# Attention: middle sums of outer operands 1 and 2 on GpSimd, and one in four long scaling rows on ScalarE

## The chip, the cores and the metric

The kernel runs on one core of a Trainium2 chip. The metric is the time of one execution in microseconds (us) on the device. All data is float32. The engines are named as in the profile: PE (TensorE, matrix products; PEld are its weight loads), DVE (VectorE), ACT (ScalarE), POOL (GpSimd) and SP (the queue that issues most of the DMAs).

## What is computed

Four sequences of 512 tokens with 1024 features are normalised, sent through causal attention and, beside it, through a linear layer with a routed low-rank part; both results are added to the input.

```python
x = hidden                                    # (4, 512, 1024)
xn = layernorm(x)
x = x + attn(xn, w_qkv, w_o) + ffn(xn, W, b, A, B, gate_w, gate_b)

def attn(h, w_qkv, w_o):                      # 32 heads, 8 key/value heads, D = 128, groups of 4
    qkv = h @ w_qkv
    scores = einsum('bqhgd,bkhd->bhgqk', q, k) * D ** -0.5
    bias = where(rel >= 0, -slopes * sqrt(max(rel, 0)), -inf)   # rel = query - key position
    attn = softmax(scores + bias)
    out = einsum('bhgqk,bkhd->bqhgd', attn, v)
    return out @ w_o
```

## The kernel before

The large matrix products (the projection by `w_qkv`, and the last stage by `w_o` and `W` together) are each made by a two-level scheme of the Strassen kind: seven products of sums of quarters in place of eight products of quarters, once over outer quarters and again over inner ones. So operands have to be summed ahead of the products. The attention stage lies between the two large products, and besides attention it makes those sums of its own output that the last stage will multiply, and stores them to HBM in `s_d`.

**Units and steps.** A unit is one key/value head `h` of one sequence 2p + bi: 2 x 8 x 2 = 32 units, and the two with the same `(p, h)` follow each other and are called a pair. A unit has NQ = 4 steps, so the loop at L1221 runs over STEPS = 128 steps and six more. One step T handles two slices of 32 queries for 4 heads at once (128 partitions). Each slice has its keys in a long and a short row of scores, which fold the causal triangle: widths 512 - 32s and 32 + 32s for slice s, so a step always has 1088 columns in four rows (`rows`, L1039; k = 0 and 2 are long, 1 and 3 short).

**What a step issues, in this order.** Every engine's order is the program's order in this stage (`manual_schedule`, L1215).

1. At T % 4 = 0 the key and query loads of the next unit (SP); at T % 4 = 2 the loads of the values, half of them on POOL's queue and half on SP's (L1035), and the bias row of the next pair (ACT).
2. Ten steps after a unit's first (T % 4 = 2 too), `settle` (L1122) copies its finished output from PSUM to `O[u]` (ACT), and its sums are put in line: see below.
3. `scores(T)`: for each row a product on PE into one of four PSUM banks, bias and row minimum on DVE (L1058, result `low`), the exponential with its row sum on ACT (L1061). After the second row DVE inverts the sums of the step before (`tot`, L1069).
4. `scaled(T - 1)`: the rows of the step before times their inverse sums, in place: the short ones on ACT (L1075), the long ones on POOL (L1077).
5. `turn(T - 2)`: DVE transposes the rows of two steps before in blocks of 32 (L1086) into `pt`.
6. In odd steps `weigh` of two steps (PE, L1102): the weighted sums of the values.
7. `aside(beside, 1)` and `aside(below, ...)`: so many sums from two lists of generators. `beside` holds sums that DVE makes, `below` those that POOL makes.

**The sums.** `outer_sums` (L1136) takes the outputs of both units of a pair and makes the outer operands 5, 6 and 3, and 7 in place, by 8 instructions of 128x512 (`HEADS`: two halves of four) on POOL. `middle_sums` (L1155) makes, from outer operands, the sums that the inner level needs: four instructions for each group, s1, s2, s4 and s3, followed by the stores into `s_d`. There are three groups per pair: operands 1 and 2 (from `O` of the even unit, 128x512, with `kept` true: s3 goes to a new place, since the quarter that it would overwrite is still used by `outer_sums`; the unchanged quarters are stored ahead of the sums, L1176 and L1177), operands 5, 6 and 3 (from `OS`, 128x768), and operands 7 and 4 (from `O` of the odd unit, 128x512). L137 and L140 are the helpers `add` and `sub`, so these instructions stand under those two lines and are told apart by their tiles: `ot` is the result of middle sums, `os` and `o` those of outer sums.

Line 1170 chooses the engine of middle sums: POOL for operands 7 and 4, DVE for the other two groups. `of_pair` (L1202) is one generator: eight outer sums, then it puts operands 5, 6 and 3 in line in `beside`, then runs operands 7 and 4 itself. The step loop takes one sum per step from `beside` and one or two (even and odd steps) from `below`: in the eight steps of a pair 8 from `beside` (4 + 4 are put in) and 12 from `below` (12 are put in). From step 128 on, up to four are taken from each per step.

At step 112 the loop also asks for the first operands of the last stage (`front[0]`, L1231, 3.2 MB on SP's queue); at step 130 for the second ones.

Of the kernel before, what the change touches and what calls it, by code (L numbers as in the profile page):

```python
# [66 lines left out]
def kernel(  # L67
# [13 lines left out]
    nc = tc.nc  # L81
# [54 lines left out]
    def add(eng, dst, u, v):  # L136
        return eng.tensor_tensor(dst, u, v, ALU.add)  # L137

    def sub(eng, dst, u, v):
        return eng.tensor_tensor(dst, u, v, ALU.subtract)  # L140
# [830 lines left out]
    def attend(front, begin):  # L971
# [3 lines left out]
        with ExitStack() as stack:  # L975
# [4 lines left out]
            STEPS = len(units) * NQ  # L980
# [10 lines left out]
            def buf(tag, name):  # L991
                where = sq if tag in queries else sp if tag in passing else sb
                return where.tile([P, *sizes[tag]], F32, tag=tag, name=name, bufs=counts.get(tag, 1))

            Q, K, V, O, bias = {}, {}, {}, {}, {}
# [4 lines left out]
            def load(u, queue=nc.sync):  # L1000
                p, h, bi = u
                n = label(u)
                K[u] = buf("k", f"k_{n}")
                Q[u] = buf("q", f"q_{n}")
                queue.dma_start(out=K[u], in_=k_d[2 * p + bi, h - h % 2][:, h % 2])
                queue.dma_start(out=Q[u], in_=q_d[2 * p + bi, h])
# [17 lines left out]
            def distances(u):  # L1024
                p, h, bi = u
                t = buf("bias", f"bias_{p}_{h}")
                nc.scalar.activation(t, dist, AF.Identity, scale=slope[:, h : h + 1])
                bias[p, h] = t

            def values(u):  # L1030
                p, h, bi = u
                V[u] = buf("v" + "xy"[bi], f"v_{label(u)}")
                src = v_d[2 * p + bi, h - h % 2][h % 2].rearrange("k g c d -> k (g c) d")
                for g in range(G):
                    (nc.gpsimd, nc.sync)[g // 2].dma_start(out=V[u][ts(g, C)], in_=src)  # L1035
# [3 lines left out]
            def rows(T):  # L1039

                for e in range(2):
                    s = 2 * (T % NQ) + e
                    high = (NB - s) * C
                    yield 2 * e, PR[T][:, e, :high], high
                    yield 2 * e + 1, PR[T][:, e, high:], (s + 1) * C
# [21 lines left out]
            def inverse(T):  # L1067
                if 0 <= T < STEPS:
                    nc.vector.reciprocal(TOT[T], TOT[T])  # L1069

            def scaled(T):
                for k, row, n in rows(T):
                    by = TOT[T][:, k : k + 1]
                    if k % 2:
                        nc.scalar.activation(row, row, AF.Identity, scale=by)  # L1075
                    else:
                        nc.gpsimd.tensor_scalar(row, row, by, 1.0, ALU.mult, ALU.mult)  # L1077
# [44 lines left out]
            def settle(u, part=slice(0, 2)):  # L1122

                if u not in O:
                    O[u] = buf("o", f"o_{label(u)}")
                for g in range(G):
                    at = slice((2 - part.stop) * HS, (2 - part.start) * HS)
                    to = O[u][:, g, part.start * HS : part.stop * HS]
                    nc.scalar.copy(
                        to.rearrange("p (j k) -> p j k", k=C)[:, ::-1],  # L1130
                        PO[u, g][:, at].rearrange("p (j k) -> p j k", k=C),
                    )
# [22 lines left out]
            def middle_sums(p, h, which, of, t, kept):  # L1155


                g = len(which)
                a = t.rearrange("p (g e) (r k) -> p g e r k", g=g, r=2) if of == "o" else t.rearrange(
                    "p g e (r k) -> p g e r k", r=2  # L1160
                )
                a11, a12, a21, a22 = [a[:, :, e, r] for r in range(2) for e in range(2)]
                n = f"{p}_{h}_{which[0]}"
                m = spare.pop(which[0]) if (p, h) == last and which[0] in spare else buf(
                    f"ot{which[0]}", f"ot_{n}"
                )
                m = m.rearrange("p (s g) k -> p s g k", g=g)
                s1, s2, s4 = [m[:, k] for k in range(3)]
                s3 = m[:, 3] if kept else a21
                eng = nc.gpsimd if of == "o" and not kept else nc.vector  # L1170
                kb, kp = divmod(h + 2, KB)

                d = [s_d[i][:, :, p, kb, kp] for i in which]
                if kept:
                    for k in range(g):
                        nc.sync.dma_start(out=d[k][:, 0:4:2], in_=a[:, k, :, 0])  # L1176
                        nc.sync.dma_start(out=d[k][:, 3], in_=a[:, k, 1, 1])  # L1177
                add(eng, s1, a21, a22)
                yield
                sub(eng, s2, s1, a11)  # L1180
                yield
                sub(eng, s4, a12, s2)
                yield
                sub(eng, s3, a11, a21)
                for k in range(g):
                    if kept:
                        nc.sync.dma_start(out=d[k][:, 1], in_=s3[:, k])
                    else:
                        nc.sync.dma_start(out=d[k][:, :4], in_=a[:, k].rearrange("p e r k -> p (e r) k"))
                    nc.sync.dma_start(out=d[k][:, 4:], in_=m[:, :3, k])  # L1190
                yield

            beside, below, spare = deque(), deque(), {}

            def aside(steps, times):
                while steps and times:
                    if next(steps[0], True):
                        steps.popleft()
                    else:
                        times -= 1  # L1200

            def of_pair(p, h, eng, cuts):  # L1202

                yield from outer_sums(p, h, eng, cuts)
                beside.append(middle_sums(p, h, (5, 6, 3), "os", OS.pop((p, h)), False))
                yield from middle_sums(p, h, (7, 4), "o", O[p, h, 1], False)
# [14 lines left out]
            for T in range(STEPS + 6):  # L1221
                n, q = divmod(T, NQ)
                done, part = divmod(T - 10, NQ)
                if q == 0 and 0 < n and n + 1 < len(units):
                    load(units[n + 1])
                if q == 2 and n < len(units):
                    values(units[n])
                    if n + 1 < len(units) and units[n + 1][2] == 0:
                        distances(units[n + 1])
                if T == 112:  # L1230
                    front[0]()  # L1231
                if part == 0 and done >= 0:
                    u = p, h, bi = units[done]
                    settle(u)
                    if bi == 0:
                        beside.append(middle_sums(p, h, (1, 2), "o", O[u], True))
                    else:
                        below.append(of_pair(p, h, nc.gpsimd, HEADS))
                if T < STEPS:
                    scores(T)  # L1240
                else:
                    inverse(T - 1)
                if 0 < T <= STEPS:
                    scaled(T - 1)
                if 1 < T <= STEPS + 1:
                    turn(T - 2)
                if T == STEPS + 2:
                    earlier.__exit__(None, None, None)
                    early.__exit__(None, None, None)
                    front[1](O[units[-2]][:, :])  # L1250
                if T == STEPS:
                    fill = begin()
                if T >= STEPS:
                    for _ in range(6):
                        next(fill, None)
                for k in range(T - 7, T - 5) if T % 2 and T < STEPS else [T - 6] if T >= STEPS else []:
                    weigh(k)
                aside(beside, 1 if T < STEPS else 4)
                aside(below, 1 + T % 2 if T < STEPS else 4)
                if T == STEPS + 4:  # L1260
                    settle(units[-1], slice(1, 2))
            for _ in fill:
# [3 lines left out]
            p, h = last  # L1266
# [473 lines left out]
    def begin():  # L1740

        bank = rotation(a=(0,), b=(1,))
        for kind, rc in (("a", (0, 0)), ("b", (0, 1))):
            begun[rc] = bank(kind, "begun")[:, :HS]
            yield from ops[0].plain(*rc, begun[rc])
# [53 lines left out]
```

## Time and profile before

| | us |
|---|---|
| runs (3): median, lowest, highest | 2529.05, 2528.04, 2530.84 |
| profiled execution | 2522.98 |
| its span, first to last instruction | 2521.2 |
| PE, DVE, POOL, ACT busy in the span | 2424.5, 1838.4, 1832.5, 590.7 |
| first and last scaling row on POOL (L1077) start at | 1139.7, 1690.1 |

The granted clock of PE is 0.991 on the mean. DMA moves 681.92 MB, 270 GB/s over the span. In the profile each instruction group is named by its line, engine, operation and tiles, with shapes as partitions x elements. "Idle before" is the time that the engine stood still ahead of an instruction, and the arrow names what ended it. A busy PE is not PE at its peak, since the products overlap; the starts on its timeline tell more than the busy time. The share of a whole run also mixes three stages with different limits (projection to 1139 us, attention, last stage from about 1700), so the attention stage is to be read by itself.

### The profile page before, as it was taken

What the parts mean: (1) busy time and instruction counts of PE and PEld (TensorE: products, weight loads), DVE (VectorE), ACT (ScalarE), POOL (GpSimd) and SP (SyncE); (2) the same over time, 40 slices, a digit from 0 to 9 for tenths busy, and PEclk for the clock granted to TensorE, in tenths of its full rate; (3) what the DMA queues carried; (4) which work ended last, traced back from release to release, by engine and by line L of the source; (5) the groups of instructions that cost most, each with busy time, mean ns of one, the idle gap of its engine ahead of it and who ended that gap; (6) DMA issues with size and microseconds to landing.
All of it is one profiled execution on the core that took longest, in us unless ns stands there. A gap on an engine that the chain in (4) does not pass through costs nothing.

```text
span 2521.2 us, 44416 instructions
## 1 busy us (share of the span) xinstructions
PE 2424.5 (96%) x16096; PEld 2067.5 (82%) x16096; DVE 1838.4 (73%) x3586; ACT 590.7 (23%) x1814; POOL 1832.5 (73%) x1876
## 2 busy tenths in 40 slices
PE   7999999999899999999999999995999999999999
PEld 6888888888788888887777777774888888888887
DVE  7776677678566676757999999976765666656574
ACT  3111111110000000018777777750000000000000
POOL 4588787877698888874888878873775667647593
PEclk9999999999999999999999999998999999999999
DMA  4389898878986777747899999999887877879884
GB/s 147 109 250 326 271 334 253 263 222 260 309 253 215 240 228 230 253 126 197 261 321 317 317 329 326 317 324 344 293 317 268 327 291 288 307 267 330 309 331 149
DMA packets 517196, 681.92 MB, mean 270 GB/s; under 512 B 155817, under 2 KB 428969, under 8 KB 502770
## 3 DMA queue, kind: packets, MB, share of 16 engines
q1 hardware_dynamic: 443122, 579.45, 69.4%
q10 hardware_dynamic: 70752, 82.85, 9.9%
q0 software_dynamic: 3104, 16.78, 2.6%
q8 instruction: 128, 2.10, 0.3%
q14 instruction: 90, 0.74, 0.1%
HBM read 417.89 MB, written 261.10 MB: 269 GB/s over the span
## 4 chain that ended last, share of the span: by engine, by line
PE 57%; DVE 6%; ACT 5%; issue 4%; DMA 2%; SPq 1%; POOL 0%; DVEq 0%; ACTq 0%; POOLq 0%
PE pc L1378 16%; PE pd L1378 8%; PE pc_q L569 7%; PE po L1102 5%; PE pa L1378 4%; PE psc L1053 4%; PE pd_q L569 4%; PE pc_kv L569 3%; ACT p L1061 3%; DVE p L1058 3%; PE pa_q L569 2%; PE pd_kv L569 2%; DVE pt L1086 2%; ACT p L1075 1%; PE pa_kv L569 1%
## 5 line engine op out<-in xcount | busy, mean ns | idle before, releaser
L1061 ACT ACTIVATE p<-p,low 128x512 f32<-128x512 f32 (+15 forms) x512 | 261.0, 514 | 134.5 <-DVE low L1058 132.5
L140 POOL TENSOR_TENSOR t<-w 128x640 f32<-128x640 f32 x95 | 183.5, 1932 | 148.4 <-DMA w<-in_w_o_dram 63.8
L1053 PE MATMUL psc<-k,q 128*128 128x512 f32 (+15 forms) x1024 | 270.4, 412 | 19.2 <-DVE low L1058 18.7
L1102 PE MATMUL po<-pt,v 32*128 32x256 f32 (+7 forms) x6144 | 280.1, 332 | 4.3 <-DMA v<-v 3.8
L1102 PEld LDWEIGHTS po<-pt,v 32*128 32x128 f32 x6144 | 255.2, 187 | 27.7 <-ACT p L1061 11.1
L1053 PEld LDWEIGHTS psc<-k,q 128*128 128x128 f32 x1024 | 170.4, 190 | 112.1 <-issue 55.0
L1077 POOL TENSOR_SCALAR p<-p,tot 128x512 f32<-128x512 f32 (+7 forms) x256 | 151.3, 603 | 122.3 <-DVE tot L1069 119.6
L140 POOL TENSOR_TENSOR t<-w,t 128x640 f32<-128x640 f32 x95 | 202.3, 2129 | 33.2 <-PE pc L1378 29.4
L1058 DVE CUSTOM_DVE_ANT_0 p<-psc,bias 128x512 f32<-128x512 f32 (+15 forms) x512 | 200.3, 426 | 22.5 <-PE psc L1053 20.5
L140 POOL TENSOR_TENSOR wr<-wr 128x256 f32<-128x256 f32 x220 | 173.8, 792 | 42.3 <-DMA wr<-in_w_o_dram 16.7
L569 PE MATMUL pc_q<-xi,ti_q 128*128 128x256 f32 x640 | 165.2, 381 | 3.5 <-DVE q L137 1.7
L1086 DVE STREAM_TRANSPOSE pt<-p 128x1088 f32<-128x1088 f32 x128 | 166.6, 1301 | 0.4 <-POOL p L1077 0.4
L140 POOL TENSOR_TENSOR ti_q<-w_q 128x256 f32<-128x256 f32 x128 | 103.7, 810 | 68.4 <-PE pc_q L569 35.7
L179 ACT COPY m<-pc 128x256 f32<-128x256 f32 x30 | 11.2, 372 | 584.1 <-PE pc L1378 577.1
L140 DVE TENSOR_TENSOR wr<-wr 128x256 f32<-128x256 f32 x220 | 139.4, 634 | 7.0 <-DMA wr<-in_wt_dram 6.2
L569 PEld LDWEIGHTS pc_q<-xi,ti_q 128*128 128x128 f32 x640 | 120.2, 190 | 23.2 <-issue 3.3
L1378 PE MATMUL pc<-sa,w 128*128 128x256 f32 x480 | 113.2, 383 | 19.9 <-DMA sa<-s 19.9
L569 PE MATMUL pd_q<-xi,ti_q 128*128 128x256 f32 x448 | 118.1, 387 | 13.8 <-POOL ti_q L140 13.5
L1378 PEld LDWEIGHTS pc<-sa,w 128*128 128x128 f32 x480 | 91.8, 193 | 32.7 <-issue 20.3
L1378 PE MATMUL pc<-s,t 128*128 128x256 f32 x480 | 113.0, 383 | 5.9 <-DVE m L137 5.9
L140 POOL TENSOR_TENSOR ti_q<-w_q,ti_q 128x256 f32<-128x256 f32 x128 | 108.4, 847 | 5.0
L1378 PE MATMUL pd<-s,t 128*128 128x256 f32 x480 | 111.4, 379 | 0.0
(349 smaller groups left out, 5848.2 us busy)
## 6 DMA issues: line engine op xcount, KB each, us to landing
sa<-s SPq DMA_DIRECT2D x98, 640.0 KB, 8.0
s<-ot SPq DMA_DIRECT2D x107, 384.0 KB, 7.0
m<-wr SPq DMA_DIRECT2D x70, 512.0 KB, 4.1
w<-m SPq DMA_DIRECT2D x28, 1280.0 KB, 7.6
w_q<-in_w_qkv_dram SPq DMA_DIRECT2D x16, 2048.0 KB, 12.0
q<-q SPq DMA_DIRECT2D x32, 1024.0 KB, 8.0
s<-os SPq DMA_DIRECT2D x48, 512.0 KB, 6.3
t<-wr SPq DMA_DIRECT2D x40, 512.0 KB, 4.2
```

The source lines that it names most:

```text
L140: return eng.tensor_tensor(dst, u, v, ALU.subtract)
L179: nc.scalar.copy(dst, alike(src, dst))
L569: nc.tensor.matmul(dst, ops_w[m][:, c, :], XI[i][m][:, c, :], start=start and c == 0, stop=c == 1, skip_group_check=True,)
L1053: nc.tensor.matmul(sc[:, :n], Q[u][:, n // C - 1].rearrange("p g k -> p (g k)"), K[u][:, :n], start=True, stop=True,)
L1058: nc.vector.tensor_tensor_reduce(row, sc[:, :n], bias[p, h][:, S - n :], -SCALE, BIG, ALU.add, ALU.min, low)
L1061: nc.scalar.activation(row, row, AF.Exp, bias=low, scale=-1.0, accum_out=TOT[T][:, k : k + 1])
L1075: nc.scalar.activation(row, row, AF.Identity, scale=by)
L1077: nc.gpsimd.tensor_scalar(row, row, by, 1.0, ALU.mult, ALU.mult)
L1086: nc.vector.transpose(dst, PR.pop(T).rearrange("p s (t k) -> p s t k", k=C))
L1102: nc.tensor.matmul(PO[u, g][:, to : to + n * C].rearrange("p (n k) -> p n k", k=C), V[u][ts(g, C), b % G * NT + b // G], x[:, :, :C], star ...
L1378: nc.tensor.matmul(bk, w[:, k], x[:, k], start=start and k == 0, stop=stop and k == KB - 1, skip_group_check=True,)
```

## The change

Three edits, all in `attend`.

```diff
@@ scaled(T), L1071
                 for k, row, n in rows(T):
                     by = TOT[T][:, k : k + 1]
-                    if k % 2:
+                    if k % 2 or k // 2 and T % 2:
                         nc.scalar.activation(row, row, AF.Identity, scale=by)
                     else:
                         nc.gpsimd.tensor_scalar(row, row, by, 1.0, ALU.mult, ALU.mult)
@@ middle_sums, L1170
-                eng = nc.gpsimd if of == "o" and not kept else nc.vector
+                eng = nc.gpsimd if of == "o" else nc.vector
@@ the step loop, L1236 and L1259
                     if bi == 0:
-                        beside.append(middle_sums(p, h, (1, 2), "o", O[u], True))
+                        below.append(middle_sums(p, h, (1, 2), "o", O[u], True))
                     else:
                         below.append(of_pair(p, h, nc.gpsimd, HEADS))
...
                 aside(beside, 1 if T < STEPS else 4)
-                aside(below, 1 + T % 2 if T < STEPS else 4)
+                aside(below, 2 if T < STEPS else 4)
```

- The second long row (k = 2) of odd steps is scaled by ACT instead of POOL: in a unit the rows of slices 3 and 7, 416 and 288 wide. The other three long rows of every two steps stay on POOL.
- The middle sums of operands 1 and 2 are issued on POOL instead of DVE, four instructions of 128x512 per pair.
- They wait in POOL's list `below`, behind operands 7 and 4 of the pair before, and that list gives two sums in every step: 16 in the eight steps of a pair, and 4 + 12 are put in. The list `beside` is left with operands 5, 6 and 3, which so start as soon as they are put in line, in steps 5 to 8 after the odd unit was settled, where they ran in steps 8 to 11.

The same arithmetic is done, and the same bytes are stored.

## Prediction

> **What bounds the kernel now.** I read the busy share of 40 slices first, to find where the edited code runs, then the table of busy time by stretch, then the timelines of PE, VectorE (DVE) and GpSimd (POOL) in that stretch, then the waits and the groups by shape. The edit touches only the attention loop, from 1139 to 1724 us.
>
> ```profile
> PE   7999999999899999999999999995999999999999
> DVE  7776677678566676757999999976765666656574
> POOL 4588787877698888874888878873775667647593
> ...
> 1225.40:1609.20 383.80, 370.01 (x4933) 290.64 (x4930) 383.66 (x969) 287.64 (x979) 311.90 (x352) 1.00 1.00 321
> ```
>
> The slices show PE full almost everywhere; only in slices 20 to 26 is DVE full as well. The last line (PE, weight loads, DVE, ACT, POOL, then clock, DMA share, GB/s) covers loop steps 24 to 111, 22 units of four steps. DVE is idle for 0.14 of 383.8 us, POOL for 72, ACT for 96. A unit takes 383.8 / 22 = 17.45 us, a pair 34.9. So DVE sets the pace here; PE's 96% has to be checked against a stretch where DVE is not full:
>
> ```profile
> 1171.64 4.28 PE L1102 MATMUL po<-pt,v 32*128 32x256 f32 x96
> 1175.85 4.27 PE L1053 MATMUL psc<-k,q 128*128 128x512 f32 x16
> 1180.05 4.31 PE L1102 MATMUL po<-pt,v 32*128 32x256 f32 x96
> 1184.29 3.93 PE L1053 MATMUL psc<-k,q 128*128 128x384 f32 x16
> 1188.16 4.28 PE L1102 MATMUL po<-pt,v 32*128 32x256 f32 x96
> ...
> 1259.93 2.32 PE L1053 MATMUL psc<-k,q 128*128 128x512 f32 x8
> 1263.00 2.16 PE L1053 MATMUL psc<-k,q 128*128 128x448 f32 x8 [0.74 <-DVE low L1058]
> ```
>
> From 1171.64 to 1188.16, before DVE has its full load, one unit takes 16.52 us with no gap: PE's own floor. Later PE waits in every unit for DVE to empty the score banks. The most that a lighter DVE can give is 17.45 - 16.52 = 0.93 us per unit.
>
> **The removed DVE work.** Per pair four sums leave DVE. Their rows in steps 24 to 111:
>
> ```profile
> L137 DVE TENSOR_TENSOR ot<-o x11: 2505/2512/2523, 1238.5 to 1587.6; 128x512 f32<-128x512 f32 x11
> L140 DVE TENSOR_TENSOR ot<-ot,o x11: 1151/1154/1157, 1243.7 to 1592.8; 128x512 f32<-128x512 f32 x11
> L140 DVE TENSOR_TENSOR ot<-o,ot x11: 1240/1244/1252, 1247.5 to 1596.6; 128x512 f32<-128x512 f32 x11
> L140 DVE TENSOR_TENSOR ot<-o x11: 1364/1366/1371, 1251.4 to 1600.5; 128x512 f32<-128x512 f32 x11
> ```
>
> 2.51 + 1.15 + 1.24 + 1.37 = 6.27 us; by starts on the timeline (instructions overlap a little) 6.06. The same sums take 0.65 each at the end of the loop, where POOL is not working beside them: most of their time is waiting for POOL. DVE falls to 34.9 - 6.06 = 28.8 us per pair, under PE's 33.04.
>
> The sums that stay on DVE (operands 5, 6 and 3; 6.85 us by starts) move three steps earlier, since their queue is no longer shared: steps 5 to 8 after the odd unit is settled, instead of 8 to 11. They stay bunched in four steps: 11.04 us of other DVE work per unit plus 6.85 is 17.9 against PE's 16.52. Bounds: 0.95 each (their fastest) gives 14.8; 2.62 each (their slowest) gives 21.5. PE covers about 3.5 us of lateness: in the PE-bound stretch DVE frees a score bank at about 1197.3 and PE needs it at 1200.8. So 17.9 is covered, 21.5 would stall PE 1.5 us per pair. I take 0.
>
> **The added POOL work.** POOL is busy 311.90 / 11 = 28.35 us per pair and waits 6.4 (its scaling row waits for DVE's `tot` 73.4 us in 1200 to 1600, 11.46 pairs).
> - Removed: four long rows, 416 and 288 wide, two of each: 2 x (604 + 524 ns) = 2.26.
> - Added: four sums. POOL's own sums of this shape show both ends: 1.27 when alone, 1.72 when a DVE sum delays them. 5.1 to 6.9.
> - Removed: two POOL sums that the departing DVE sums delay, 2 x 0.45 = 0.9, or nothing if others delay them.
>
> Sum: 30.3 to 33.0 us per pair. Even the upper end is just inside PE's 33.04, with no room for waits. I take the middle, 31.6, because only four DVE sums are left to delay sixteen POOL sums. A step now has two sums and 1 or 2 rows; the pace of sums (2 x 8) equals their supply (4 + 12), so no queue grows. Rows reach the transpose late only if POOL is over 2.7 us behind (row done 1195.5, transposed 1198.25); behind the row waits the transpose, and all of DVE behind that. In the pace above POOL lags by 1 to 2 us, when the two V loads that it issues (1.04 us per unit) and a contended sum fall together.
>
> GPSIMD Engine Reference (Trainium skill), section "Performance versus the Vector engine", speaks against the move: an elementwise add of two tensors is 1.96 times slower there, so "use DVE for elementwise". The rows give 1.27 against 0.65 without company, the same ratio, and by that the change adds 2.5 us of work per pair; but by the rows with company DVE gives up 6.06 and POOL takes 5.1 to 6.9, so the ratio does not decide.
>
> **ACT.** It gains the four rows. No 416- or 288-wide scaling is in the trace; the nearest rows are its exponentials of those widths, 626 and 520 ns, so 2.29 per pair, on 26.1 now: 28.4 of 33.04. Bounds: hidden, or wholly on the path, 2.29 per pair. I take hidden: the rows come after the step's exponentials, and on the timeline ACT waits 0.9 to 2.3 us for `low` in three steps of four. In the first steps that cover is missing (ACT 9.66 of 10 us busy from 1140 to 1150): three rows there, 2 x 0.63 + 0.52 = 1.8 us lost.
>
> **Queues and DMA.** No DMA is added. The four loads-out of unchanged quarters move two steps later; the last ones stay in their step but now wait for POOL's sum, which ends up to 3.5 us into the next step. Behind them on SP's queue stand the V loads, which have five steps (some 20 us) less about 7 to land: cost nothing. If that cover goes, the price is seen at step 116:
>
> ```profile
> 1636.28 1.40 SPq L1035 DMA_DIRECT2D v<-v  x2
> ...
> 1643.40 1.19 PE L1102 MATMUL po<-pt,v 32*128 32x256 f32 x2 [3.00 <-DMA v<-v]
> ...
> 1645.35 6.38 PE L1102 MATMUL po<-pt,v 32*128 32x256 f32 x90 [0.76 <-DMA v<-v]
> ```
>
> There the block of 96 took from 1639.70 to 1651.66, 11.96 us instead of 4.21. The six stores ahead of that V load (1619.88 to 1636.1) are the ones that move three steps earlier, so 0 to 7.75 us may come back. I take 0: from 1640 to 1757 DMA is at a share of 1.0, PE waits 20 us for `sa` loads at the end of it, and what PE gains earlier it would wait longer there.
>
> The bytes set a floor too: 321 GB/s x 383.8 us = 123.2 MB. In stretches of 10 us with a share of 1.0 or more the rates are 324 to 365, mean about 339; 123.2 MB at 339 is 363 us, 16.5 per unit, level with PE. The small DMA gaps that are left (0.83 to 0.96 in one such stretch of three) would have to close. DMA: Bandwidth & Descriptors (Trainium skill), section "Specifications", puts HBM at about 358 GB/s per core; at that, by estimate, the floor were 344 us and DMA would leave 4% to spare, which no long stretch here shows.
>
> **Sum.** PE and DMA both allow 16.5 per unit; I take 16.7, adding 0.2 for the DMA gaps and the bunched DVE sums. 23 units (steps 24 to 115) x (17.45 - 16.70) = 17.2, less 1.8 at the start: 15.4 us off the profiled 2521.2 span (2522.98 with what lies around it). That execution is 6.1 under the median of the runs, 2529.05; I take the difference from the median: **2513.6**. Own range: at 16.52 with nothing lost 21 to 25, at 17.0 only 8: 2505 to 2521.
>
> **Rivals.**
> 1. *All comes back* (0.13): 23 x 0.93 = 21.4 and the 7.75 at step 116: 2500. For it: the stores move ahead of the load. Against: DMA full behind it.
> 2. *Transfers set the pace* (0.15): DMA's share is already 1.00 at 321 GB/s. If 327 is all that it sustains, 123.2 MB take 377 us: 7 saved, 1.8 lost, 2524; at 321, 2531. I put it at 2525. Against: 20-us stretches at 339 to 345.
> 3. *GpSimd sets the pace, slower* (0.17): its waits for `tot` are not slack if DVE, held back by denser POOL work, gives `tot` later. With contended sums (33.0) and half the waits kept (3.2) a pair takes 36.2, 1.3 more: x 11.5 = 15, near 2544. It decides from about 2 us of waits kept on top of 33. For it: the 2.5-us sums show DVE held through two POOL instructions. Against: two sums per step leave POOL behind `tot`, not ahead of it, and after two-sum steps it does not wait today.
>
> That the edit does nothing has no place: its three lines change engines and pace in every pair.
>
> **Chances.** Forecast 0.55. Faster by over 0.2% (5 us, about what a measurement here can tell): 0.55 + 0.13 + a third of rival 2, 0.72; within: 0.11; slower: 0.17. The range 2500 to 2533 leaves out most of rival 3 and the lower half of rival 1.
>
> **What would show it.** Right: DVE's busy time in steps 24 to 111 falls from 100% to about 87%, units near 16.7 us, POOL at 94% with waits for `tot` under 1.5 us per pair, DMA above 330 GB/s. Wrong: units over 17.4, transposes waiting for `p` of L1077 or L1075, remaining DVE sums over 2.5 us each, PE waiting for v, q or k in more places than step 116.

## The result, and the profile after

| | before | after |
|---|---|---|
| runs (4 each): median, lowest, highest | 2529.08, 2528.04, 2530.84 us | 2549.78, 2543.44, 2552.03 us |
| profiled execution, its span | 2522.98, 2521.2 us | 2549.02, 2547.2 us |
| steps 24 to 111 | 383.6 us, 17.44 per unit | 403.4 us, 18.33 per unit |

The kernel became **slower by 0.8%**: the ratio of times is 1.0077 (interval 1.0058 to 1.0096). The forecast of 2513.6 us was wrong in sign, and the time lies outside its range.

The busy shares of the 40 slices after the change, in tenths:

```profile
PE   7999999999899999999999999985999999999999
DVE  7776676678576667657777877775765766655574
POOL 4588787786698989876888988874765667656593
```

DVE has lost its full slices 20 to 26, as forecast, and POOL is fuller there. By that row alone the change works. The table of the stretch from 1225.40 to 1609.20 us (length, then busy PE, weight loads, DVE, ACT, POOL, then clock, DMA share, GB/s) says otherwise:

```profile
1225.40:1609.20 383.80, 358.44 (x4684) 280.18 (x4680) 299.78 (x888) 294.62 (x977) 327.33 (x337) 0.96 0.98 308
```

DVE is busy for 78%, POOL for 85%, PE for 93%, and transfers fell from 321 to 308 GB/s: none of these engines is full, and all have less to do per microsecond. So something late holds them all. What that is, the longest waits of PE, DVE and POOL from 1225 to 1600 us show (total us, times, longest):

```profile
DVE p L1058 <- PE psc L1053: 76.6, 39, 7.6
POOL p L1077 <- DVE tot L1069: 42.8, 19, 6.3
PE psc L1053 <- DMA q<-q: 12.6, 5, 5.1
PE psc L1053 <- issue: 10.8, 3, 4.7
```

DVE waits for PE now. POOL's waits for `tot` went down from 68.4 us in the same stretch, where rival 3 needed them to decide. PE itself waits for a load of queries, for which it never waited here before; on its timeline (start, duration, instruction, idle before):

```profile
1226.81 4.27 PE L1053 MATMUL psc<-k,q 128*128 128x512 f32 x16
1231.01 4.31 PE L1102 MATMUL po<-pt,v 32*128 32x256 f32 x96
1235.25 3.93 PE L1053 MATMUL psc<-k,q 128*128 128x384 f32 x16
1239.11 4.28 PE L1102 MATMUL po<-pt,v 32*128 32x256 f32 x96
1248.11 6.47 PE L1053 MATMUL psc<-k,q 128*128 128x512 f32 x16 [4.72 <-issue]
...
1321.63 7.25 PE L1053 MATMUL psc<-k,q 128*128 128x512 f32 x16 [3.58 <-DMA q<-q]
```

Step 24 starts at 1226.81. Its unit runs at PE's floor and would end at 1239.11 + 4.28 = 1243.39; step 28 starts at 1248.11, and its 16 products take 6.47 us in place of 4.27. That wait bears the name "issue": the trace names nothing that ended it. Five waits at the same place in other units are named `q`, and SP's queue shows the query load of step 28 late as well:

```profile
1225.15 0.91 SPq L1189 DMA_DIRECT2D s<-os  x1
1226.10 0.91 SPq L1190 DMA_DIRECT2D s<-ot  x1
1227.05 0.59 SPq L1189 DMA_DIRECT2D s<-os  x1
1228.33 0.52 SPq L1190 DMA_DIRECT2D s<-ot  x1
1228.89 1.63 SPq L1189 DMA_DIRECT2D s<-os  x1
1230.57 3.14 SPq L1190 DMA_DIRECT2D s<-ot  x1
1233.80 0.86 SPq L1005 DMA_DIRECT2D k<-k  x1
1234.71 0.45 SPq L1006 DMA_DIRECT2D q<-q  x1
```

Keys and queries have two buffers, so the load of the next unit can go only when the last scores of the unit before are made, 3.7 us ahead of step 24 (in step 16 it went then, with nothing in front of it). Here the query load went 7.9 us into the step, behind the six stores of operands 5, 6 and 3 (3 x (512 + 384) KB). A query load takes 9.0 us to land at the median and 12.3 at most (7.4 and 8.9 before; the trace has the landing of six loads in each kernel), and the unit that it must be ready for could start 16.5 us after step 24.

**Where the time went.** The two executions differ by 26.0 us of span: 1.4 before step 24, 19.8 in steps 24 to 111, 4.1 from there to the end of the wait for `sa` that opens the last stage (at 1784.24 against 1758.97; the wait is 21.79 us against 19.93), and 0.7 behind it. In steps 24 to 111 the load of the next unit goes behind the stores of 5, 6 and 3 in every second unit, eleven of 22. In five of these (steps 24, 40, 56, 72 and 88) it went 7.0 to 8.3 us into the step: they take 18.1 to 21.7 us, together 19.8 over a floor of 16.515, and the five units after them 10.0 over it. All 22 are 40 over.

### The profile page after: what moved, and what is told of

It is laid out like the page before. It is cut to its first block, busy times and chain, and to the rows that moved or that the text cites. A ratio compares the mean times of both kernels' runs of the same rounds, so it can differ in the third digit from the quotient of the medians.

```text
span 2547.2 us, 44424 instructions
## 1 busy us (share of the span) xinstructions
PE 2432.1 (95%) x16096; PEld 2070.5 (81%) x16096; DVE 1754.7 (69%) x3522; ACT 620.0 (24%) x1878; POOL 1881.4 (74%) x1876
## 4 chain that ended last, share of the span: by engine, by line
PE 48%; DMA 7%; SPq 3%; POOL 3%; ACT 2%; issue 2%; DVE 2%; DVEq 0%; POOLq 0%; ACTq 0%
PE pc L1378 16%; PE pd L1378 8%; PE psc L1053 5%; PE po L1102 5%; PE pa L1378 4%; PE pc_q L569 4%; DMA q<-q 3%; PE pd_q L569 2%; PE pc_kv L569 2%; SPq L1190 1%; ACT p L1061 1%; DMA s<-o 1%; DMA s<-ot 1%; PE pa_q L569 1%; DVE p L1058 1%
## 5 line engine op out<-in xcount | busy, mean ns | idle before, releaser
L1053 PE MATMUL psc<-k,q 128*128 128x512 f32 (+15 forms) x1024 | 279.4, 426 | 41.7 <-DMA q<-q 23.6
L1058 DVE CUSTOM_DVE_ANT_0 p<-psc,bias 128x512 f32<-128x512 f32 (+15 forms) x512 | 202.4, 432 | 127.4 <-PE psc L1053 119.0
L1053 PEld LDWEIGHTS psc<-k,q 128*128 128x128 f32 x1024 | 175.6, 198 | 139.1 <-issue 93.7
L1077 POOL TENSOR_SCALAR p<-p,tot 128x512 f32<-128x512 f32 (+2 forms) x192 | 116.5, 615 | 97.4 <-DVE tot L1069 86.6
L1075 ACT ACTIVATE p<-p,tot 128x32 f32<-128x32 f32 (+4 forms) x320 | 121.4, 439 | 0.0
L1378 PEld LDWEIGHTS pc<-sa,w 128*128 128x128 f32 x480 | 91.8, 193 | 35.6 <-issue 22.2
```

The costliest lines, as they stand in the source:

```text
L1053: nc.tensor.matmul(sc[:, :n], Q[u][:, n // C - 1].rearrange("p g k -> p (g k)"), K[u][:, :n], start=True, stop=True,)
L1058: nc.vector.tensor_tensor_reduce(row, sc[:, :n], bias[p, h][:, S - n :], -SCALE, BIG, ALU.add, ALU.min, low)
L1378: nc.tensor.matmul(bk, w[:, k], x[:, k], start=start and k == 0, stop=stop and k == KB - 1, skip_group_check=True,)
```

## The experiments

Three theories were set against each other. O: the **order** on SP's queue, stores issued ahead of the key and query loads. D: the **transfers** as a whole are too many or too dense, whatever their order. P: **GpSimd** sets the pace. O2 and P2 are the forms that O and P took after the first four runs. A ratio is to the kernel before, run beside them on the same chip (its medians there were 2527.77, 2527.99 and 2527.65 us for the three batches).

To follow O, call S the step in which a pair's odd unit is settled (S % 8 = 6). Key and query loads go out in steps S + 2, S + 6 and S + 10. Before, the stores of (7, 4) were issued from step S + 7 and those of (5, 6, 3) from S + 11, each just **behind** a load. With two sums in every step and `beside` left to (5, 6, 3), they are issued from S + 5 and S + 8, **ahead** of the loads of S + 6 and S + 10.

### First batch: undo one part, or do one part alone

**The sums of 5, 6 and 3 three steps later**, the rest as changed:

```diff
-                beside.append(middle_sums(p, h, (5, 6, 3), "os", OS.pop((p, h)), False))
+                beside.append(later(3, middle_sums(p, h, (5, 6, 3), "os", OS.pop((p, h)), False)))
```

> The changed kernel with one part undone: the sums of operands 5, 6 and 3 start three steps later, in steps 8 to 11 after the odd unit was settled as before the change; their six stores then stand on SP's queue ahead of a V load again and no longer ahead of a key and query load. Theory O (order: the query load of every second unit lands late because those stores were moved right in front of it): the waits for q (23.6 us named in the changed kernel's profile) go to under 3 us, a unit takes 16.5 to 17.0 us, total 2508 to 2520. Theory D (capacity: at PE's pace the transfers can't be served, whatever their order): loads stay late, total 2540 or more. Theory P (POOL runs late, its sums hold up SP's queue): no change, 2545 to 2552.

Measured: 2546.81 us (2540.16 to 2549.03), ratio 1.0070 (1.0054 to 1.0086). The number is D's and P's, and not O's. SP's queue shows why:

```profile
1357.76 0.38 SPq L1189 DMA_DIRECT2D s<-o  x1
1358.18 0.51 SPq L1190 DMA_DIRECT2D s<-ot  x1
1358.79 1.16 SPq L1189 DMA_DIRECT2D s<-o  x1
1359.99 1.24 SPq L1190 DMA_DIRECT2D s<-ot  x1
1361.33 1.19 SPq L1005 DMA_DIRECT2D k<-k  x1
1362.57 1.11 SPq L1006 DMA_DIRECT2D q<-q  x1
```

The load behind (5, 6, 3) goes in time now, but the other load, of S + 6, goes behind the four stores of (7, 4), and PE waits there:

```profile
1373.63 5.93 PE L1053 MATMUL psc<-k,q 128*128 128x512 f32 x16 [2.47 <-DMA q<-q]
```

One of two groups was out of the way and the loss moved to the other. The run doesn't tell O from D or P; it said that both groups must be dealt with.

**Key and query loads on ACT's queue**, past all stores:

```diff
-                    load(units[n + 1])
+                    load(units[n + 1], nc.scalar)
```

> The changed kernel with the key and query loads issued on ACT's queue instead of SP's, stores left where they are. Theory O: the load is no longer behind the six stores on its queue, but shares the DMA engines with them: waits for q under 8 us, total 2510 to 2525. Theory D: loads stay late, 2540 or more. Theory P: SP's waits for POOL no longer hold the load, 2510 to 2525 as well; so this run with the one before tells P from O.

Measured: 2517.63 us (2514.41 to 2521.38), ratio 0.9960 (0.9947 to 0.9973). The same work and the same bytes, in the same order but for these two loads, and 32 us less: no wait for `q`, 16.83 us per unit (mean of the 22 units from step 24 on, here and below), and transfers at 334 GB/s where the changed kernel had 308. That speaks for O, and against D: denser transfers went faster.

**The scaling edit alone** (the kernel before, with its line 1074 as changed):

```diff
-                    if k % 2:
+                    if k % 2 or k // 2 and T % 2:
```

> The kernel before with the scaling edit alone (one in four long rows on ACT). DVE keeps all its sums, so the unit stays near 17.4 us: total 2525 to 2531 under all theories (1.8 us lost in the first steps on ACT, up to 3 won where DVE's sums find POOL idle).

Measured: **2502.59 us** (2502.06 to 2507.71), ratio 0.9904 (0.9890 to 0.9919). Missed: 25 us faster where none were expected. Its table for the same stretch:

```profile
1225.40:1609.20 383.80, 383.80 (x5172) 304.54 (x5170) 374.99 (x1024) 326.76 (x1079) 306.42 (x326) 1.00 1.04 337
```

PE never stops: units of 16.515 us, its floor, with the middle sums still on DVE. 337 GB/s held over 383.8 us ends rival 2 and D. DVE is busy for 375 us of 384, with the work of 23.2 units where it had that of 22. The sums by shape (least/median/most ns) show how it found the room:

```profile
L137 DVE TENSOR_TENSOR ot<-o x12: 1759/1766/1776, 1237.3 to 1600.6; 128x512 f32<-128x512 f32 x12
L140 DVE TENSOR_TENSOR ot<-o,ot x12: 647/650/651, 1245.7 to 1609.0; 128x512 f32<-128x512 f32 x12
L137 DVE TENSOR_TENSOR ot<-os x11: 1484/1499/1505, 1253.8 to 1584.1; 128x768 f32<-128x768 f32 x11
L140 DVE TENSOR_TENSOR ot<-os,ot x12: 914/917/919, 1229.2 to 1592.5; 128x768 f32<-128x768 f32 x12
```

The four took 2.51, 1.24, 2.61 and 1.51 us before; the other four of a pair kept their times within 0.02. That is 0.75 + 0.59 + 1.11 + 0.59 = 3.04 us per pair, 1.5 per unit, off an engine that was full: 17.45 - 1.5 = 15.9 (and 374.99 / 23.2 = 16.1), below PE's 16.5. POOL runs one row fewer in odd steps, so the DVE sum that stands waiting behind POOL's rows is released a row earlier. First before, then with the scaling edit:

```profile
1238.03 1.22 POOL L1077 TENSOR_SCALAR p<-p,tot 128x448 f32<-128x448 f32 x2
1238.52 2.52 DVE L137 TENSOR_TENSOR ot<-o 128x512 f32<-128x512 f32 x1
1239.23 1.26 POOL L140 TENSOR_TENSOR os<-os,o 128x512 f32<-128x512 f32 x1
...
1236.60 0.65 POOL L1077 TENSOR_SCALAR p<-p,tot 128x448 f32<-128x448 f32 x1
1237.21 1.27 POOL L140 TENSOR_TENSOR os<-os,o 128x512 f32<-128x512 f32 x1
1237.27 1.78 DVE L137 TENSOR_TENSOR ot<-o 128x512 f32<-128x512 f32 x1
```

In both, the DVE sum ends 0.55 to 0.57 us after POOL's sum does. Before, it had also stood through what was left of two rows.

**The moved sums without the scaling edit** (the changed kernel, L1074 as before):

```diff
-                    if k % 2 or k // 2 and T % 2:
+                    if k % 2:
```

> The changed kernel without the scaling edit: all long rows on POOL, which then has 2.26 us more per pair. Theories O and D: within 4 us of the changed kernel, 2543 to 2554, since the loads decide. Theory P: slower than the changed kernel by up to 2.26 x 11.5 = 26 us, 2560 or more.

Measured: 2564.05 us (2559.15 to 2565.13), ratio 1.0144 (1.0127 to 1.0161). The number is P's. But PE again waits for `q`, and SP stands for 91.7 us waiting for POOL's `o` ahead of stores (84.6 in the changed kernel): POOL, with more to do, makes the sums later, and the loads behind their stores go later still. So P seems to have a part in the size, through the queue of O (the second batch takes this up).

### Second batch: is it the order?

**Stores of both groups issued just behind the key and query load** (the changed kernel; `stores` holds the six lines of L1185 to L1190, and `holding` is true up to step 116):

```diff
+                if kept or not holding[0]:
+                    stores()
+                else:
+                    held.append(stores)
...
+                if q == 0:
+                    while held:
+                        held.pop(0)()
+                holding[0] = T < 116
```

> The changed kernel, same engines and same sums at the same steps; only the stores of operands 7 and 4 and of 5, 6 and 3 are issued behind the next key and query load on SP's queue (one and two steps later) instead of ahead of it. Theory O2 (any group of stores that stands ahead of a key and query load holds it back, first until its last sum is done and then by its own transfer; with the change both groups stand there, and undoing one only moved the late load to the other): waits for q under 3 us in steps 24 to 111, a unit 16.5 to 16.9 us, total 2505 to 2522. Theory P2 (the lag of POOL stalls PE and DVE directly, the late loads are a sign of it): the total stays over 2535.

Measured: 2523.43 us (2518.67 to 2525.10, 10 runs), ratio 0.9979 (0.9969 to 0.9988). In steps 24 to 111 the loss is gone:

```profile
1225.40:1609.20 383.80, 380.59 (x5146) 301.66 (x5145) 323.67 (x959) 320.52 (x1068) 357.52 (x368) 1.00 1.03 334
```

A unit takes 16.77 us, no wait for `q` is left, DVE is at 84% and POOL at 93%. What is left above the floor stands in the odd units of the pairs (16.9 to 17.3 us, the others 16.5). In ten of these eleven DVE waits 1.6 to 2.5 us ahead of its first sum of 5, 6 and 3, seven times by name for stores that still read that buffer (`DVE ot L137 <- DMA s<-ot: 14.8, 7, 2.5`). With the loads on ACT's queue, where no store is held, such waits stand in the odd units too (nine), so the holding alone does not explain them; no run separates this rest. The time missed O2's range by a microsecond for one wait of 11.26 us ahead of step 124 (at 1666.82), after the holding has ended and while the operands of the last stage are loaded.

**The pace alone, on the scaling edit alone**: nothing is moved to POOL, only `below` gives two sums in every step, so that (7, 4) come two steps earlier:

```diff
-                aside(below, 1 + T % 2 if T < STEPS else 4)
+                aside(below, 2 if T < STEPS else 4)
```

> The kernel before with the scaling edit, and with two sums per step from POOL's list as in the change, but no sum changes its engine: operands 7 and 4 are then done and stored two steps earlier, ahead of a key and query load. POOL's work is the same as in the scaling edit alone (2502.6). Theory O2: late loads in every second unit, q waits of 10 us or more in 1225 to 1600, total 2520 to 2545. Theory P2: POOL has the room, so 2500 to 2508.

Measured: **2579.51 us** (2577.97 to 2584.37), ratio 1.0206 (1.0191 to 1.0222): 77 us slower than without this line. P2 is refuted; O2's direction is right and its size far too small. SP's queue and PE (the step began at 1323.52):

```profile
1323.52 2.58 SPq L1035 DMA_DIRECT2D v<-v  x2
...
1328.60 1.02 SPq L1189 DMA_DIRECT2D s<-o  x1
1329.66 0.56 SPq L1190 DMA_DIRECT2D s<-ot  x1
1330.26 1.52 SPq L1189 DMA_DIRECT2D s<-o  x1
1331.83 0.94 SPq L1190 DMA_DIRECT2D s<-ot  x1
1332.86 1.16 SPq L1005 DMA_DIRECT2D k<-k  x1
1334.06 1.41 SPq L1006 DMA_DIRECT2D q<-q  x1
```

```profile
1336.17 4.28 PE L1102 MATMUL po<-pt,v 32*128 32x256 f32 x96
1344.60 6.75 PE L1053 MATMUL psc<-k,q 128*128 128x512 f32 x16 [4.16 <-DMA q<-q]
```

The query load goes 10.5 us into the step and PE stands still for 4.16. With the scaling edit alone, the same two loads stand ahead of the four stores (the step began at 1307.63):

```profile
1312.98 0.52 SPq L1005 DMA_DIRECT2D k<-k  x1
1313.55 1.44 SPq L1006 DMA_DIRECT2D q<-q  x1
...
1319.12 1.06 SPq L1189 DMA_DIRECT2D s<-o  x1
...
1322.60 1.38 SPq L1190 DMA_DIRECT2D s<-ot  x1
```

Read off such timelines for all 22 units from step 24 on, from the start of a unit to the query load issued in it, for the later loads (every second unit), and the length of that unit in us:

| kernel | the later of the loads | that unit | the other units |
|---|---|---|---|
| before | 5.8 to 6.8 us (eleven) | 17.3 | 17.2 to 17.6 |
| scaling edit alone | 5.6 to 6.8 us (eleven) | 16.5 | 16.5 |
| changed kernel | 7.0 to 8.3 us (five), 5.0 to 6.9 (six) | 18.1 to 21.7, 16.5 to 19.0 | 17.1 to 19.5 |
| scaling edit and pace | 9.2 to 10.5 us (eleven) | 19.8 to 21.6 | 17.2 to 19.7 |

With the scaling edit alone 6.8 us costs nothing; from 7.0 on PE waits every time. In between it hangs on the landing: in the changed kernel four of the six loads at 5.0 to 6.9 us were followed by waits of 0.7 to 2.4 us, and two of these four took 11.5 and 12.3 us to land. So before the change the later loads had little to spare already. A unit after a long one is mostly long too.

**The scaling edit with key and query loads on ACT's queue** (both lines are shown above):

> The kernel before with the scaling edit, and the key and query loads on ACT's queue. No stores stand ahead of these loads in the steady steps, so both theories expect little there: 2498 to 2506; the one q wait near step 116 (behind the operands of the last stage) goes, up to 5 us.

Measured: 2530.76 us (2524.65 to 2537.04, 10 runs), ratio 1.0011 (1.0001 to 1.0020). Missed by 25 us. On this order the loads were in time anyway, and on ACT they hold up its exponentials: in step 48, which began at 1318.84, the first one starts only behind the query load.

```profile
1323.90 0.33 ACTq L1006 DMA_DIRECT2D q<-q  x1
1324.35 0.72 ACT L1061 ACTIVATE p<-p,low 128x512 f32<-128x512 f32 x1 [4.66 <-DVE low L1058]
```

Its input `low` was made by 1320.8. The waits of 1225 to 1600 us:

```profile
POOL p L1077 <- DVE tot L1069: 90.7, 43, 4.4
ACT p L1061 <- DVE low L1058: 45.9, 36, 5.0
...
DVE tot L1069 <- ACT p L1061: 20.9, 10, 2.8
```

DVE, which has only 9 us to spare here, waits 20.9 us for ACT. So that queue is not a free way round: it took 32 us off the changed kernel and put 28 on this one. DMA: Bandwidth & Descriptors (Trainium skill), section "Issuing engines are not separate DMA queues", says that issuing from several engines saves only the sequencer's time of issuing, usually small. Here what is saved is the time that a load stands behind stores and their waits, 2549.78 against 2517.63 us, and it is not small; that no rate is won agrees, with 334 GB/s at most on two queues and 334 to 337 on SP's alone in the kernels without waits for `q`.

**The moved sums without the scaling edit, loads on ACT's queue:**

> The change without its scaling edit, key and query loads on ACT's queue. What is left of the loss here is not the queue's: theory O2 expects 2515 to 2530 (POOL has 2.26 us more per pair than with the scaling edit, where the same queue gave 2517.6), theory P2 2540 or more.

Measured: 2525.86 us (2522.05 to 2533.40, 10 runs), ratio 0.9996 (0.9983 to 1.0009), as O2 expected: 38 us under the same kernel with the loads on SP. POOL is busy for 374.08 us of 383.8, 97%, and still no slower than before. With these loads on ACT's queue, leaving out the scaling edit costs 8.2 us (2525.86 against 2517.63), on SP's 14.3: so P seems to have a part of its own, some 8 us, beside the one through the queue.

### Third batch: one group at a time, and a better kernel

**The pace alone, on the kernel before** (the one line of the pace, nothing else):

> The kernel before with two sums per step from POOL's list as the only edit. Theory O2: the stores of operands 7 and 4 stand ahead of a key and query load, so q waits in every second unit, though at the slower pace of 17.45 us per unit there is more time for each load: 2540 to 2575. If the order of these stores did not matter, 2525 to 2531.

Measured: 2586.70 us (2585.67 to 2593.02), ratio 1.0240 (1.0225 to 1.0255). No sum and no row changes its engine, and the kernel loses 59 us, more than expected: 36.6 us of waits for `q`, nine of them, in 1225 to 1600 us, at a granted clock of 0.94. That is about three times the loss of the whole change by the line that the prediction priced at nothing.

**The scaling edit and the pace, with the stores of (7, 4) alone put behind the load:**

> The slow kernel of the second batch (scaling edit, two sums per step, no sum on another engine; 2579.5) with one difference: the four stores of operands 7 and 4 are issued one step later, behind the key and query load instead of ahead of it. The sums run at the same steps on the same engines. Theory O2: back to the scaling edit alone, 2500 to 2512, no q waits in steps 24 to 111. If the earlier sums themselves cost the time (POOL denser, DVE held longer), 2560 or more stays.

Measured: 2521.51 us (2517.99 to 2523.02, 10 runs), ratio 0.9975 (0.9966 to 0.9985). 58 of the 77 us come back by issuing four stores later, and no wait for `q` is left. The rest, expected back too, did not come: a unit takes 17.04 us, with DVE at 364.5 of 383.8. Unlike with the scaling edit alone, PE waits once per unit for DVE here (`PE psc L1053 <- DVE low L1058: 6.3, 22, 0.4`), and POOL stands 21.1 us for PE ahead of its V loads. What holds the remaining half microsecond was not taken apart: 58 of the 77 us are the order of these stores, for 19 the cause is open.

**The scaling edit, with the operands of the last stage asked for one at a time** in steps 112, 116, 120 and 124:

```diff
-                if T == 112:
-                    front[0]()
+                if T in (112, 116, 120, 124):
+                    front[0]((*QUARTERS[:3], "w")[(T - 112) // 4])
```

> The scaling edit alone (2502.6), and the first operands of the last stage are asked for one by one at steps 112, 116, 120 and 124 instead of all at step 112. The 6.5 us wait for v at step 116 and the slower products behind it should go: up to 9 us, 2493 to 2502; if the transfers behind it only move the wait to the last stage, 2500 to 2504.

Measured: **2500.67 us** (2499.12 to 2502.29), ratio 0.9894 (0.9879 to 0.9909), the fastest of all. The wait for `v` at step 116 (6.5 us with the scaling edit alone) is gone, but PE then waits 3.47 us for `w` and still 19.22 us for `sa` ahead of the last stage (19.08 with the scaling edit alone): only some 2 us are won, as transfers are full there (a share of 1.01 from 1609 to 1760 us).

**The whole change, stores behind loads up to step 124, operands spread:**

> The whole change with its stores behind the loads up to step 123, and the operands spread over the same four steps: what the change is worth when no store stands ahead of a key and query load, at the end of the loop either. Theory O2: 2503 to 2514 (units of 16.76 us as in the held kernel, the 11 us wait for q near its end gone). It should not beat the scaling edit alone.

Measured: 2507.51 us (2505.91 to 2511.38), ratio 0.9922 (0.9906 to 0.9939), as expected. With the order mended the change is worth 20 us over the kernel before, and still costs 7 against the scaling edit with the same spread: 16.77 us per unit against 16.515, with DVE again waiting for stores ahead of those sums (14.2 us by name).

## Why the prediction was wrong

**What bounds the kernel: right.** DVE did set the pace before: 3 us per pair off it put PE on its floor, and the floor is the 16.5 us that was read off the timeline.

**Removed DVE work: right in size, not needed.** With the order mended DVE is busy for 84% where 87% was forecast. But 1.5 us per unit, half of what was taken off, is enough. (The 0.65 us of a sum without company stand at the start of the loop, from 1171 to 1184 us, not at its end, where the rows are 0.68 to 0.69.)

**Added POOL work: right.** 31.6 us per pair were forecast; with the stores held POOL has 357.52 / 383.8 x 33.54 = 31.2, in the changed kernel 31.3. The prediction weighed GPSIMD Engine Reference (Trainium skill), section "Performance versus the Vector engine", against the move and set its ratio of 1.96 aside. The rows support this: with the stores held the four sums cost POOL 1.28 + 1.58 + 1.31 + 2.00 = 6.2 us (means by shape, the first three over the groups (1, 2) and (7, 4)), in company with DVE's, and DVE gave up 6.06.

**The scaling edit: its term was mis-sized.** It was priced as 2.26 us of POOL's work per pair, hidden on ACT. The rows that leave POOL also release DVE's waiting sums, 3.04 us per pair on the engine that sets the pace: 25 us alone. The prediction had the fact in hand (2.51 in company, 0.65 without) and used it for the sums that move, not for those whose neighbours go. The 1.8 us that ACT was to lose in the first steps were not lost: from step 0 to step 24 it is 91.8 us before and with the scaling edit alone.

**Queues and DMA: here it failed.** The step said of the moved stores that the V loads stand behind them on SP, with five steps to spare, "cost nothing". The V loads did have that cover. But the key and query loads of T % 4 = 0 stand behind those stores too, and were not named. They have two buffers, so one unit of 16.5 us from the start of the step, and 7.4 to 9 of it go for landing. The count that failed is of *what the queue issues next*, not of bytes: the bytes went at 337 GB/s when PE let them. Its price: in the whole change 26 us or more (2549.78 against 2523.43 with the stores held), and 58 of the 77 us that the pace costs on the scaling edit. The 59 us of the pace alone were not split.

**The stall at step 116.** Taken as unchanged. The wait for `v` did go, and waits for `q` of 3.18 and 5.78 us came ahead of steps 116 and 120: from step 112 to 124 it is 63.2 us where it was 59.2, so 4 us worse where zero was taken.

**Rivals.** 2 (transfers) fell with 337 GB/s. 3 (GpSimd, 2544) came within 6 us of the time, but not by its mechanism: waits for `tot` fell, and POOL was 85% busy. Of the signs that were to show the forecast wrong two came: units over 17.4 us (18.33), and "PE waiting for v, q or k in more places than step 116", which names the cause.

**Two sums of the prediction** are a little off and change nothing: 344 us against 363 leave 5% to spare, not 4, and the chances for faster add up to 0.73.

**Left open.** A third buffer for keys and queries, or stores on a queue of their own, would attack the same wait and were not tried. Why one unit after a long one is long too, with its loads in time, was only argued: after most waits of over 2 us 16 products take 5.8 to 7.3 us, and the loads that follow are pushed behind the next stores.

## What to carry to other kernels

When work is moved along a hand-ordered program, write down for every transfer that it issues which loads it now stands ahead of on that queue, and for each of these loads its slack: the buffers less one, times the period, less the landing at its slowest (here 16.5 less 9 to 12 us, counted from the start of the step). Issue the load with the least slack first and let stores follow. And where two engines hold each other up, take the smallest piece off the one that holds, and measure it alone before more is moved.

## What was not expected of the hardware

- A sum on DVE is held through more than one POOL instruction: 0.65 us without POOL's company, 1.77 with one scaling row fewer ahead of it, 2.51 with both. A row of 0.5 to 0.6 us taken off POOL gave the DVE sum behind it 0.75.
- After PE had stood still for some 2 to 6 us, its next 16 products mostly took 5.8 to 7.4 us where 4.27 is usual (4.24 after one wait of 3.18), and the granted clock of the stretch fell from 1.00 to 0.96 in the changed kernel and to 0.94 with the pace alone. In the run with the sums of 5, 6 and 3 later it was 0.71 over the 5.9 us behind a wait of 1.86. A late load can cost its wait and some 3 us more.
- With the two loads of each unit issued on ACT's queue, DVE waited 20.9 us in 375 for ACT's exponentials.
